# A mixture-of-experts block after a state-space layer: rows stored ready for the experts, and a start ordered around the first batch's norm

## The chip, the cores and the metric

The kernel runs on one core of a Trainium2 chip. A core has five engines with queues of their own: PE (matmuls), DVE (vector), ACT (scalar, with tables for functions), POOL (GpSimd) and SP (which only issues DMAs); PEld is PE's weight load. The metric is the device time of one execution in microseconds; less is better. A profile is one execution with its instructions recorded.

## The reference

All data are float32. x has 8 batches of 512 rows (tokens) with D = 256 features. A small matrix product of a condition `c` gives six vectors per batch: shift, scale and gate for each half of the layer.

```python
mod = (silu(c) @ wmod).reshape(8, 6, 1, 256)      # sa, ca, ga, sb, cb, gb
ga, gb: sign kept, magnitude at least 0.25
h = layernorm(x) * (1 + ca) + sa
# first half, a state-space layer with its own norm and residual
xn = layernorm(h) * gamma + beta
xp, z = split(xn @ W_in.T)                        # 512 + 512 features
xc = silu(causal_depthwise_conv(xp, 4 taps) + conv_b)
s_t = s_{t-1} @ A.T + xp_t @ Bm.T                 # 16 states, over the 512 rows
y = (xc + s @ Cm) * sigmoid(z)
x = x + ga * (h + y @ W_out.T)
# second half, eight experts, one for each token
h = layernorm(x) * (1 + cb) + sb
p = softmax(h @ wr + br); e = best expert; gate = p1 / (p1 + p2)
x = x + gb * gate * (gelu(h @ w1[e] + b1[e]) @ w2[e] + b2[e])
```

## The kernel before, in words

**Stages.** The first part goes over the eight batches. For each: `stage_norm` (both norms of x, then transposes to `xnT`, features on the partitions), `stage_base` (the residual `base` and the output weights `wb_` times the gate, both on POOL), `stage_conv` (the state scan by `pv`, `pd`, `v`, and the convolution: projections `px`, copies to `u`, three taps on DVE into `sv`), `stage_out` (projections for z, the states' part `pc`, then `po`: output projection and router logits together, giving the new x, `x1`), and `stage_place` (which expert, gate, and where among its expert's tokens each row goes: the row numbers are scattered to `ids_d` by indirect DMA). Ahead of the batches come general preparations: `states()` (powers of A and tables made of them, in many small matmuls and copies) and `vectors()` (the six vectors for all batches as rows, written to DRAM as `mod_d` and `modb_d`; by feature in `modT` through the tile `pf`; products of them with the router's weights). Batch 0's first three vectors are made apart, in `bc0`.

The second part goes over blocks of 256 rows of one expert (slots; some single ones of 128): weights `w1t`, `w2t`, biases `b1t`, `b2t`, the rows' numbers `ids`, and the rows `xg`, gathered from the DRAM table `xp_d` by indirect DMA. `features` makes the second norm's output `hg` on DVE and transposes it to `hT`; `layer1` gives `gl` by `ph` and Gelu; `layer2` gives `py`, then `ot` on DVE, which is scattered to the output. Four slots (`NEARLY`) are formed from the first six batches (`FEW`), and slot 0's rows and weights are fetched while the batches still run. The last three single slots run only if they are filled.

**A row of the table** holds 1028 numbers: the 256 of x1, the norm's 1/sigma and -mean/sigma, the gate, a zero (`OWN` = 260), then the batch's three vectors of the second half, which DMAs of 1.5 MB per batch copy from `modb_d` to every row, DRAM to DRAM.

**Order.** The kernel's text doesn't set the order of instructions. A class `Plan` records them, with estimated lengths, what each depends on, the buffers of its tiles and a due time (`nc.due`; `PERIOD` = 36 us a batch, `SLOT` = 14.5 us), passes due times back along dependencies, and then builds the queues in a loop that always takes the instruction that could start first, the earlier due one where two are equal:

```python
                    if best is None or (at, o["due"]) < best[:2]:
                        best = (at, o["due"], o)
```

What it takes is written out to the engines' queues in that order, and each queue runs strictly in order. `nc.wanting(done=...)` adds a dependency to the plan alone, `wanting([tile])` a buffer that must be free. There are two plans, one for each part. Line 154 is where a matmul that continues a group is recorded, line 159 any other instruction; so nearly all lines of the profile carry one of these two numbers, and tiles tell them apart.

**Other names.** `sv` (two buffers) holds the convolution and then y of a batch; `normed` is four ACT operations on [128, 256]; `stats` is bn_stats and bn_aggr on DVE, then `rs` by a power on POOL and `nm`; `late` (new) is a list of DMAs that the second part issues. The constant tables `sl_at`, `ex_at`, `seen` and `prio` are filled by one-element memsets on POOL.

Of the kernel before, what the change touches and what calls it, by code (L numbers as in the profile page):

```python
# [10 lines left out]
FP = mybir.dt.float32  # L11
# [10 lines left out]
OWN = 260  # L22
# [13 lines left out]
class Plan:  # L36
# [20 lines left out]
    def __init__(self, tc, last=None):  # L57

        self.tc, self.nc = tc, tc.nc
        self.free = {q: last.free[q] if last else 0.0 for q in self.REACH}  # L60
        self.ops, self.touched, self.tiles = [], {}, {}
        self.due, self.also, self.pairing = 0.0, ([], []), 0
        for name in self.QUEUES:
            setattr(self, name, self.Engine(self, name))
# [71 lines left out]
    def add(self, name, op, args, kw):  # L136
# [19 lines left out]
        else:  # L156
# [6 lines left out]
            self.ops.append(me)  # L163
        if op == "activation":
            me["table"] = {AF.Gelu: 1, AF.Silu: 2, AF.Tanh: 2}.get(args[2] if len(args) > 2 else None)
        if "dma" in op:
            me["size"] = 4
            for _, n in out.ap:
                me["size"] *= n
            me["indirect"] = "indirect" in op  # L170
# [20 lines left out]
    def order(self):  # L191
# [19 lines left out]
        order, table = [], 2  # L211
# [14 lines left out]
        while len(order) < len(ops):  # L226
            best = None
            for q, l in ready.items():
                for o in l:
# [6 lines left out]
                    if best is None or (at, o["due"]) < best[:2]:  # L236
                        best = (at, o["due"], o)
            assert best is not None, "no buffer for any instruction that could be next"
            at, _, o = best
            table = o.get("table") or table  # L240

# [6 lines left out]
            free[o["queue"]] = at + o["length"]  # L248
            end = at + o["length"]
# [40 lines left out]
def adaln_mamba_moe_kernel(  # L290
# [89 lines left out]
    for e in range(E):  # L380
        nc.gpsimd.memset(seen[0:1, e : e + 1], float(e * TOK))
# [4 lines left out]
    for i in range(NSLOT):  # L386
        single = i >= NPAIR
        m = i - NPAIR if single else i
        for q, v in enumerate((
            m, NPAIR + m // 2 if single else m, (m % 2) * P if single else 0,  # L390
            0 if single else NSING,
        )):
            nc.gpsimd.memset(sl_at[:, q, i : i + 1], float(v))

    ex_at = cpool.tile([1, 2, 2 * E], FP, name="ex_at")
    for e in range(2 * E):
        nc.gpsimd.memset(ex_at[:, 0, e : e + 1], float(e % E))
        nc.gpsimd.memset(ex_at[:, 1, e : e + 1], float((e % E) * TOK))
# [5 lines left out]
    ROW = OWN + 3 * D  # L404
    ids_d = dpool.tile([NIDS, 1], I32, name="ids_d")
    id_views = dram_disjoint_views(ids_d, NB)
    xp_d = dpool.tile([TOK + BLK, ROW], FP, name="xp_d")
# [6 lines left out]
    xg0 = epool.tile([P, JB, ROW], FP, name="xg0", tag="xg0")  # L414
    zero = xg0[:, 0, :]
# [15 lines left out]
    with tc.tile_pool(name="wa", bufs=1) as wa, tc.tile_pool(  # L431
# [3 lines left out]
    ) as a2, tc.tile_pool(  # L435
        name="rowp", bufs=2
# [27 lines left out]
        cmt = wa.tile([DS, DI], FP, name="cmt")  # L464
# [5 lines left out]
        for j in range(JB):  # L470
            nc.sync.dma_start(out=xp_d[TOK + j * P : TOK + (j + 1) * P, :], in_=zero)
# [41 lines left out]
        def vectors():  # L513

            for half, to in ((0, mod_d), (1, modb_d)):
                mod = wa.tile([B, 3, D], FP, name=f"mod{half}", tag="mod")
                three(mod, sT, half, B)
                nc.sync.dma_start(out=to, in_=mod.rearrange("b i d -> b (i d)"))


            pf = ps_o.tile([P, 6, B], FP, name="pf", tag="po")
            for m in range(6):
                w, at_m = (wmh[1], m) if m < 4 else (wmh[0], m)
                for k in range(KD):
                    nc.tensor.matmul(
                        pf[:, m], lhsT=w[:, k, at_m * P : (at_m + 1) * P],
                        rhs=sT[:, k, :], start=(k == 0), stop=(k == KD - 1),
                    )
            nc.vector.tensor_copy(modT[:, 0:2], pf[:, 0:2])
            nc.vector.tensor_scalar(modT[:, 2:4], pf[:, 2:4], 1.0, None, ALU.add)  # L530
            gT = modT[:, 4:6]
            nc.vector.tensor_copy(gT, pf[:, 4:6])
            mT = wa.tile([P, KD, B], FP, name="mT")
            nc.vector.scalar_tensor_tensor(mT, gT, -1.0, gT, ALU.mult, ALU.max)
            nc.vector.tensor_scalar(mT, mT, 0.25, None, ALU.max)
# [853 lines left out]
```

## Time and profile before

| | us |
|---|---|
| median of 3 runs | 591.7 (588.8 to 591.74) |
| the profiled execution | 587.33 |
| its span, first to last instruction | 585.2 |
| PE busy | 562.3 |
| DVE, ACT, POOL busy | 348.1, 211.0, 209.3 |
| first `po` of batch 0, of batch 7 (chain of waits) | 71.83, 305.51 |
| mean granted clock of PE | 0.987 |

In the page's rows of tenths each character is one of 40 equal slices of the span (14.6 us), 9 meaning 90% or more. In the windows view each engine has its busy microseconds and its count of instructions in brackets, then come the granted PE clock, the DMA share and GB/s. A timeline line has start, duration, engine, line, operation, tiles (out<-in), sizes and count, and in brackets the idle time before it and what ended it.

### The profile page before, as it was taken

Reading aid. Unit: us, or ns where it says so; the run is one execution under the profiler, and the core shown is the slowest. Engines: PE = TensorE matmul, PEld = TensorE weight load, DVE = VectorE, ACT = ScalarE, POOL = GpSimd, SP = SyncE. Lnnn points to the kernel's source line nnn. Section 1 sums busy time; section 2 is a strip of 40 time slices with the busy share of each in tenths; the row PEclk is TensorE's granted clock in tenths of the full one; section 3 lists DMA queues with packets and bytes.
Section 4 is the critical chain, followed back from the end, with each engine's and each line's share of the span. In section 5 each row is a group of like instructions: output and inputs, shape, how many; then the busy total and the mean of one; then the engine's idle time right before and its main releaser. Section 6 shows DMA issues by size and latency. Waiting matters only on the chain.

```text
span 585.2 us, 8673 instructions
## 1 busy us (share of the span) xinstructions
PE 562.3 (96%) x2882; PEld 428.0 (73%) x2882; DVE 348.1 (59%) x1087; ACT 211.0 (36%) x404; POOL 209.3 (36%) x330
## 2 busy tenths in 40 slices
PE   4999999999999999999999798999999999999996
PEld 2454766757576676757578687878988988988895
DVE  4879968798987968686595924163433433522312
ACT  2328454455363445252342021222422222332140
POOL 1423673635446372621333421342242222322112
PEclk9779999999999999999999999999999999999999
DMA  7348999420210101010553969997887787886000
GB/s 277 129 129 183 271 254 258 71 91 0 64 38 1 38 2 36 1 37 1 161 175 91 239 198 398 394 396 266 282 279 275 274 251 242 276 286 194 15 18 20
DMA packets 58703, 96.73 MB, mean 165 GB/s; under 512 B 9852, under 2 KB 41854, under 8 KB 58656
## 3 DMA queue, kind: packets, MB, share of 16 engines
q1 hardware_dynamic: 50720, 72.98, 41.4%
q0 software_dynamic: 7936, 23.17, 11.1%
q8 instruction: 24, 0.39, 0.3%
q14 instruction: 23, 0.19, 0.2%
HBM read 86.42 MB, written 22.81 MB: 187 GB/s over the span
## 4 chain that ended last, share of the span: by engine, by line
PE 73%; DMA 17%; DVE 3%; issue 3%; SPq 1%; POOL 1%; ACT 0%; POOLq 0%; ACTq 0%
PE py L154 10%; PE px L159 10%; PE po L154 9%; PE px L154 9%; DMA out<-ot,ids 8%; PE ph L159 6%; PE ph L154 6%; PE pc L154 3%; PE po L159 3%; PE pd L154 3%; DMA ids<-ids_d 3%; DMA ids_d<-tok,row 2%; DMA w1t<-in_w 2%; PE py L159 2%; DMA xg<-xp_d,ids 1%
## 5 line engine op out<-in xcount | busy, mean ns | idle before, releaser
L159 ACT ACTIVATE gl<-ph,b1t 128x256 f32<-128x256 f32 (+1 forms) x152 | 68.3, 452 | 179.5 <-PE ph L154 159.9
L154 PE MATMUL py<-w2t,gl 128*128 128x256 f32 x476 | 108.3, 379 | 0.0
L154 PEld LDWEIGHTS py<-w2t,gl 128*128 128x128 f32 x476 | 90.4, 190 | 12.3
L159 PE MATMUL ph<-hT,w1t 128*128 128x256 f32 (+1 forms) x304 | 84.1, 358 | 5.4 <-DMA w1t<-in_w 3.0
L154 PE MATMUL ph<-hT,w1t 128*128 128x256 f32 (+1 forms) x304 | 83.8, 357 | 0.0
L159 POOL DMA_INDIRECT out<-ot,ids x36 | 36.4, 1012 | 130.7 <-DVE ot L159 121.0
L159 DVE TENSOR_TENSOR ot<-py,b2t 128x256 f32<-128x256 f32 x34 | 14.4, 424 | 113.0 <-PE py L154 113.0
L159 DVE SCALAR_TENSOR_TENSOR sv<-u,pt,sv 128x512 f32<-128x512 f32 x96 | 71.9, 759 | 4.3 <-ACT sv L159 4.3
L159 POOL DMA_INDIRECT xg<-xp_d,ids x36 | 38.9, 1080 | 87.3 <-DMA ids<-ids_d 48.3
L159 PE MATMUL px<-xnT,wi 128*128 128x512 f32 x128 | 69.6, 625 | 0.0
L154 PE MATMUL px<-xnT,wi 128*128 128x512 f32 x128 | 66.2, 599 | 0.0
L159 PEld LDWEIGHTS ph<-hT,w1t 128*128 128x128 f32 x304 | 54.4, 190 | 12.2 <-issue 3.6
L154 PEld LDWEIGHTS ph<-hT,w1t 128*128 128x128 f32 x304 | 55.3, 190 | 6.2
L154 PEld LDWEIGHTS px<-xnT,wi 128*128 128x128 f32 x128 | 24.6, 192 | 31.2 <-issue 31.2
L159 POOL DMA_INDIRECT ids_d<-tok,row x32 | 34.5, 1077 | 24.2 <-DVE row L159 13.2
L159 ACT COPY u<-px 128x512 f32<-128x512 f32 x32 | 18.7, 585 | 67.0 <-PE px L154 66.4
L159 ACT ACTIVATE tz<-px 128x512 f32<-128x512 f32 x32 | 19.0, 595 | 51.1 <-PE px L154 50.3
L159 POOL TENSOR_TENSOR rs<-ve,nhalf 128x4 f32<-128x4 f32 x16 | 18.8, 1174 | 44.9 <-DVE ve L159 32.2
L159 PEld LDWEIGHTS px<-xnT,wi 128*128 128x128 f32 x128 | 21.3, 192 | 17.4 <-issue 16.5
L159 DVE COPY hT<-tp 128x512 f32<-128x512 f32 (+1 forms) x20 | 12.7, 634 | 35.4 <-PE tp L154 27.4
L159 DVE TENSOR_TENSOR xr<-po,h 128x256 f32<-128x256 f32 x32 | 13.5, 423 | 30.6 <-PE po L154 30.4
L159 DVE TENSOR_TENSOR hg<-hg,xg 128x256 f32<-128x256 f32 x72 | 29.3, 421 | 1.1
(347 smaller groups left out, 949.8 us busy)
## 6 DMA issues: line engine op xcount, KB each, us to landing
w1t<-in_w SPq DMA_DIRECT2D x19, 1024.0 KB
w2t<-in_w SPq DMA_DIRECT2D x19, 1024.0 KB
xp_d<-modb_d SPq DMA_DIRECT2D x8, 1536.0 KB
xp_d<-xr SPq DMA_DIRECT2D x8, 520.0 KB
xt<-in_x SPq DMA_DIRECT2D x8, 512.0 KB
bc<-mod_d SPq DMA_DIRECT2D x7, 384.0 KB
b2t<-in_b SPq DMA_DIRECT2D x19, 128.0 KB
w<-in_w SPq DMA_DIRECT2D x2, 1024.0 KB
```

Of the source, the lines that this page charges most:

```text
L154: me["calls"].append(lambda: getattr(getattr(self.nc, name), op)(*args, **kw))
L159: calls=[lambda: getattr(getattr(self.nc, name), op)(*args, **kw)],
```

## The change

- **What a row holds.** A row of `xp_d` becomes three times 256 numbers: x1, the second norm's finished output h2, and gg, which is gate times gb. They are made per batch in `stage_place`: h2 by four `normed` operations on ACT and two multiplications or additions of [128, 1024] on POOL, gg by four ACT operations; both lie in the batch's `sv`, which is now in a pool of its own (`yp`, two buffers). The three vectors come by one load `bb` per batch (one buffer). This work is due one `PERIOD` later than the rest of its batch. The last batch's h2 and gg are written by the second plan, behind slot 1's weights. The 1.5 MB copies of vectors go.
- **Experts.** `features` only transposes; `layer2` has two DVE operations on both tiles ahead of the matmuls and two per tile behind them, where there were three per tile. All four early slots are gathered in the first plan (there were two).
- **Start.** `stage_norm(0)` is recorded first, due at 20 us; `vectors()` is planned behind its `xnT`. `pf` is made by six transposes of `mod`'s rows, where there were 24 matmuls and seven DVE operations. Small copies in `states()` go from DVE to ACT.
- **Planner.** Up to 24 us (`hold`) an engine takes the earliest due of what could start within 0.3 us. Up to 100 us (`thick`) PE takes a dense instruction, if there is one within 0.3 us, when few columns were streamed in the last 3.4 us. Up to 20 us (`warm`) a PE that would wait gets filler matmuls of the identity, 256 columns each, into a tile that nobody reads.
- **Constants.** 116 one-element memsets become four iotas, some copies and some 15 memsets.

The diff, cut to its core:

```diff
@@ Plan.order
+                if could:
+                    mine = min(could)
+                    if mine[0] < self.hold:
+                        mine = min((c for c in could if c[0] < mine[0] + 0.3), key=lambda c: c[1:3])
+                    if q == "PE" and mine[0] < self.thick:
+                        t, l = mine[0], mine[3]["length"]
+                        lately = sum(
+                            d * max(0.0, b - max(a, t + l - 3.4)) / (b - a) for a, b, d in streamed[-40:]
+                        )
+                        if lately + mine[3]["dense"] < 1800:
+                            dense = [c for c in could if c[3]["dense"] > 900 * c[3]["length"] and c[0] < t + 0.3]
+                            mine = min(dense, key=lambda c: c[1:3]) if dense else mine
...
+            if self.warm and o["queue"] == "PE" and at < self.warm[0]:
+                slow = 2 if at < self.warm[1] else 1
+                n = int(0.8 * (at - free["PE"]) / (slow * self.warm[2]))
+                if n > 0:
+                    order.append(dict(i=-1, at=free["PE"], queue="PE", calls=[self.warm[3]] * n))
+                    streamed.append((free["PE"], at, 512 * n))
...
@@ vectors
+            pf = ps_o.tile([P, 6, B], FP, name="pf", tag="po")
             for half, to in ((0, mod_d), (1, modb_d)):
+                nc.due = (1 + 2 * half) * PERIOD
+                mod = rowp.tile([B, 3, D], FP, name=f"mod{half}", tag="bb", bufs=1)
                 three(mod, sT, half, B)
                 nc.sync.dma_start(out=to, in_=mod.rearrange("b i d -> b (i d)"))
+                for m, i in ((0, 1), (2, 0)) if half else ((4, 2),):
+                    for k in range(KD):
+                        nc.tensor.transpose(
+                            pf[:, m + k], mod[:, i, k * P : (k + 1) * P], ident[0:B, 0:B]
+                        )
+            nc.due = 3 * PERIOD
+            nc.vector.tensor_copy(modT, pf)
@@ states (and 13 more like it)
-                nc.vector.tensor_copy(at[:, j + 1], pa)
+                nc.scalar.copy(at[:, j + 1], pa)
@@ stage_place
+            own = xp_d[b * L : (b + 1) * L].rearrange("(n p) (i d) -> i p n d", p=P, i=3)
+            nc.sync.dma_start(out=own[0], in_=x1)
...
-            nc.sync.dma_start(
-                out=xp_d[b * L : (b + 1) * L, 0:OWN].rearrange("(n p) c -> p n c", p=P), in_=xr
-            )
-            for n in range(b + 1 if b else 0, min(b + 2, B)):
-                nc.sync.dma_start(
-                    out=xp_d[n * L : (n + 1) * L, OWN:ROW], in_=modb_d[n].partition_broadcast(L)
-                )
+            nc.sync.dma_start(
+                out=bb, in_=modb_d[b].rearrange("(i d) -> i d", d=D).partition_broadcast(P)
+            )
+            nc.due += PERIOD
+            normed(h2, x1, rs, nm)
+            nc.gpsimd.tensor_tensor(h2, h2, rows(bb[:, 0, :]), ALU.mult)
+            nc.gpsimd.tensor_tensor(h2, h2, rows(bb[:, 1, :]), ALU.add)
+            if b < B - 1:
+                nc.sync.dma_start(out=own[1], in_=h2)
+            for n in range(NT):
+                nc.scalar.activation(
+                    gg[:, n, :], bb[:, 2, :], AF.Identity, scale=gt[:, n, :]
+                )
+            if b < B - 1:
+                nc.sync.dma_start(out=own[2], in_=gg)
+            else:
+                late.extend(((own[1], h2), (own[2], gg)))
+            nc.due -= PERIOD
@@ features
-                nc.vector.tensor_scalar(
-                    hg[:, j, :], xg[:, j, 0:D], xg[:, j, D : D + 1], xg[:, j, D + 1 : D + 2],
-                    ALU.mult, ALU.add,
-                )
-                nc.vector.tensor_tensor(hg[:, j, :], hg[:, j, :], mg[:, j, 0:D], ALU.mult)
-                nc.vector.tensor_tensor(hg[:, j, :], hg[:, j, :], mg[:, j, D : 2 * D], ALU.add)
@@ the order of the start
+        plan.hold, plan.thick = 24.0, 100.0
+        plan.warm = (20.0, 7.8, 0.47, lambda: chip.tensor.matmul(
+            pwarm, lhsT=ident, rhs=twice, start=True, stop=True
+        ))
+        nc.due = 20.0
+        t = stage_norm(0)
+        nc.due = 1e6
         cs, wb, lm, bw = states()
-        rw, rsum, wr2 = vectors()
+        with nc.wanting(done=[t["xnT"]]):
+            rw, rsum, wr2 = vectors()
+            nc.due = 3 * PERIOD
+            stage_base(t)
@@ the early slots
+                for i in range(NEARLY):
+                    pre.append(rows_of(
+                        i, epool.tile([P, JB, 3, D], FP, name=f"xg_{i}", tag=f"xg{i}"), (b + 1) * L
+                    ))
@@ the second plan
+        for to, v in late:
+            with nc.wanting(done=[got[1][4]]):
+                nc.sync.dma_start(out=to, in_=v)
@@ layer2
+            nc.vector.tensor_tensor(
+                ot[:, 0:jb], gg, b2t.unsqueeze(1).to_broadcast([P, jb, D]), ALU.mult
+            )
+            nc.vector.tensor_tensor(x1, x1, ot[:, 0:jb], ALU.add)
...
-                nc.vector.tensor_tensor(ot[:, j, :], py, b2t, ALU.add)
-                nc.vector.tensor_tensor(ot[:, j, :], ot[:, j, :], mg[:, j, 2 * D : 3 * D], ALU.mult)
-                nc.vector.scalar_tensor_tensor(
-                    ot[:, j, :], ot[:, j, :], xg[:, j, D + 2 : D + 3], xg[:, j, 0:D],
-                    ALU.mult, ALU.add,
-                )
+                nc.vector.tensor_tensor(ot[:, j, :], py, gg[:, j, :], ALU.mult)
+                nc.vector.tensor_tensor(ot[:, j, :], ot[:, j, :], x1[:, j, :], ALU.add)
```

## The prediction

> **What bounds the kernel now.** I read the page first: which engine is full, and in which slices.
>
> ```profile
> span 585.2 us, 8673 instructions
> PE 562.3 (96%) x2882; PEld 428.0 (73%) x2882; DVE 348.1 (59%) x1087; ACT 211.0 (36%) x404; POOL 209.3 (36%) x330
> ...
> PE   4999999999999999999999798999999999999996
> ...
> PEclk9779999999999999999999999999999999999999
> DMA  7348999420210101010553969997887787886000
> ```
>
> PE is full almost everywhere, so only three things can pay: PE work removed, PE time at a low granted clock, and the few slices below 9 (the first, the 23rd and 24th, the last). The PEclk row has two sevens right at the start. Next the windows view, cut by stage, to see what those places are worth.
>
> ```profile
> core 0: us, PE busy (x) PEld busy (x) DVE busy (x) ACT busy (x) POOL busy (x), PEclk, DMA share, GB/s
> 0.00:10.00 10.00, 2.60 (x17) 0.93 (x17) 5.45 (x34) 1.50 (x2) 2.73 (x24) 1.00 0.74 262
> 10.00:20.00 10.00, 10.00 (x57) 6.32 (x56) 6.19 (x23) 3.15 (x6) 0.10 (x1) 1.00 0.88 330
> 20.00:30.00 10.00, 10.00 (x42) 3.05 (x42) 7.79 (x27) 4.51 (x8) 7.05 (x7) 0.66 0.01 2
> 30.00:40.00 10.00, 9.11 (x33) 5.82 (x32) 8.65 (x34) 1.95 (x3) 3.09 (x9) 0.70 0.53 141
> 40.00:50.00 10.00, 10.00 (x58) 4.95 (x56) 6.84 (x17) 6.26 (x10) 3.93 (x3) 0.95 0.61 146
> ...
> 80.00:313.00 233.00, 231.47 (x1220) 156.77 (x1213) 184.54 (x593) 103.78 (x182) 101.35 (x192) 1.00 0.26 70
> 313.00:345.00 32.00, 28.81 (x142) 24.71 (x141) 21.19 (x102) 7.36 (x17) 13.01 (x13) 1.00 0.74 183
> 345.00:388.00 43.00, 39.75 (x187) 33.77 (x186) 15.72 (x37) 11.38 (x24) 13.73 (x14) 1.00 1.05 383
> 388.00:550.00 162.00, 162.00 (x818) 143.99 (x817) 60.10 (x148) 45.81 (x102) 44.60 (x42) 1.00 0.76 256
> ```
>
> From 80 to 313 us (the batches) PE idles 1.5 us in 233; from 388 to 550 (the experts) not at all. DVE is at 79% in the batches and 37% in the experts, so DVE work taken from the experts' stage buys nothing there. What is left is the start (0 to 80) and the hand-over between the stages (313 to 388), where PE idles 6.4 us and DMA stands at 0.74 and 1.05. Last, the timeline of the start: when do inputs land, and when does batch 0 reach its projections?
>
> ```profile
> 5.64 1.41 DVE L159 BATCH_NORM_STATS2 st<-xt 128x6 f32<-128x256 f32 x4 [1.21 <-DMA xt<-in_x]
> 9.98 2.08 PE L159 MATMUL pm<-wm,s 128*128 128x512 f32 x2
> 10.20 0.14 DVE L159 SCALAR_TENSOR_TENSOR nm<-mv,rs 128x4 f32<-128x4 f32 x1
> 24.24 2.07 ACT L159 ACTIVATE xn<-h,nm,rs 128x256 f32<-128x256 f32 x4 [1.63 <-DVE nm L159]
> 37.48 2.05 PE L159 MATMUL px<-xnT,wi 128*128 128x512 f32 x2
> ```
>
> x of batch 0 is there at 5.6 us, its second norm ends at 26.3, yet the first projection starts at 37.5: PE spends the time between on general preparations. And two 128x512 matmuls take 2.05 to 2.08 us here; their median in the tile's own rows is 592 ns each, overlapping. They run at half rate.
>
> **The change part by part.**
>
> *Start, clock.* PEclk of 0.66, 0.70 and 0.95 in the three windows from 20 to 50 us is 0.34+0.30+0.05 of 10 us: 6.9 us of PE lost. The record says 1.00 before 20, but pm at 9.98 runs at half speed too; dense work began at 7.97 and pg of 15.09 us is fast again, so another 2 to 3 us. The change puts filler matmuls on the waiting PE from about 2 us (ident is ready at 1.7), and up to 100 us of the plan prefers dense PE work when the last 3.4 us were thin. The Trainium skill (TensorE: Matmul & The Clock Gate, Part 1) says that the ramp penalty is under 1% of a typical span and should not be fitted: by the rule under 5.9 us, paid once. The trace shows the clock falling back twice more, 6.9 plus about 2.5 us, 1.6% of the span. I go by the trace: 9.4 us to be had. Fillers run only where the planner expects an idle PE; a misjudged input costs one batch of fillers, 1 to 2 us.
>
> *Start, PE work.* pf loses 24 matmuls (2.6 us, of 16.05 to 18.80) for six small transposes; the start-to-start of tp transposes is 0.11 us, so 0.7: 1.9 us gained. Together 11.3 us of PE time.
>
> *Start, order.* Batch 0's norm is due first. By the rows above: stats to 7.6, rs on POOL 1.04, nm at 8.9 (no longer behind a copy of `at`: it went at 10.20 because that copy waited for PE), xn 2.1, two h operations 2.4, stats and rs 3.8, xn 2.1, transposes and xnT 2: projections from about 22 us instead of 37.5. That alone is worth nothing, since PE was busy; it lets dense work fill the stretch in which it was thin. All of `vectors()` now waits for xnT in the plan: mod_d, written at 33.3, may come later by some us, and batch 1's bc with it; batch 1's projections are not needed until 80, so this is covered by 40 us.
>
> *Start, other engines.* 35 copies of 16x16 to 128x128 size go from DVE to ACT: 35 x 0.155 = 5.4 us off DVE, and about 35 x 0.2 (the row of gt, 128x4, 0.20 us) = 7 us onto ACT. DVE was at 10.00 and 9.61 of 10 from 50 to 70 us, behind the sv taps, and a start that is 11 us shorter gives it less time: 53 us of DVE work from 10 to 80 become about 47 in 58. It fits, but not without bubbles. 116 one-element memsets of POOL at 0.09 us (10 us) go; nobody waited for them: nothing. I take 8 of the 11.3 us, bounds 2 and 13.
>
> *Batches.* Per batch, normed(h2) adds four ACT operations (2.07 us by the row of xn) and gg four more (2.1): ACT from 103.8/233 = 45% to 57%. POOL gets two multiplications of 128x1024, 2.35 us each by the rows of h: 43% to 58%. Nobody on PE waits for h2 or gg of the same batch. What is queued behind them: on POOL the ids_d scatters and the next base, on ACT u and sv copies, each late by one operation at most, 0.5 us (ACT) or 2.35 (POOL). But DVE and POOL share a port. The row is
>
> ```profile
> 28.83 2.41 POOL L159 TENSOR_TENSOR h<-h,xt 128x1024 f32<-128x1024 f32 x1
> ...
> 28.95 2.31 DVE L159 COPY lx<-more 16x16 f32<-16x16 f32 x1
> ```
>
> a 16x16 copy that takes 0.155 elsewhere and here lasts as long as the POOL operation. The skill (SBUF — State Buffer, Who interferes with whom) says the loser blocks fully until the other ends: by the rule 16 x 2.35 = 37.6 us of DVE could go, 4.7 per batch. Over the 24 such POOL operations of this trace I add up the excess of each overlapped DVE operation over its usual length: 15.8 us, 0.66 each. I take 16 x 0.66 = 10.6 us on DVE, 1.3 a batch: 79% becomes 84%, still below PE. To PE passes what falls into the scan (v, pd, v), where PE waits for DVE: I take +1 us, bounds 0 and +10.6.
>
> SP: per batch the 1536 KB DRAM broadcasts and the 520 KB rows become three writes of 512 KB and a 384 KB load. The broadcasts held SP's queue for 30 us from 42.7 and DMA at 1.02 from 60 to 80, but nothing on PE waited: nothing. sv is now held until h2 and gg are written (see rivals).
>
> *Hand-over.* PE's idle stretches here, by the timeline: 0.99 (w1t of slot 1), 2.21 (ACT waiting for b1t), 2.04 (w1t of the third weights, 12.4 us under way at DMA 1.05) and 1.1 in bits at 383 to 387 (rows of slot 4). Rows of slots 2 and 3 (four gathers of 526 KB, 2.1 MB) move ahead of 313, into a stage with DMA at 0.26; each later gather is a quarter smaller; against it, 1 MB of h2 and gg of the last batch comes in after slot 1's weights instead of a 520 KB write. Net over 1.5 MB less at 383 GB/s: 4 us of transfer. But h2 of the last batch needs ACT 2.1 and POOL 4.7 behind the four scatters that end at 327.6: about 333; SP stands in order before it, while slot 4's ids load waits for ids_d until 340.4 anyway, 7 us of cover. I take -2 us, bounds -5 and +4.
>
> *Experts and tail.* Of DVE six operations of a two-tile slot leave features and two leave layer2, and two that span both tiles come: covered by PE at 162 of 162, nothing; with the cover gone it would be 2 to 3 us a slot. Only behind the last py does one stand free: three operations (0.42+0.42+0.48) become two, -0.5.
>
> Sum: -8 +1 -2 -0.5 = -9.5, from the profiled execution's 587.33 (span 585.2): 577.8. The median shown, 591.7, is 4.4 above that execution; from it the same gain gives 582.2.
>
> **The rivals.**
>
> *A: PE keeps the whole start.* Only the clock and pf count, nothing is lost to DVE, the hand-over closes: -11.3 -5 -0.5 = -17, about 575. For it: 9.4 us are recorded. Against it: DVE at 10 of 10 from 50 to 70.
>
> *B: the start is given back in the batches.* If the port's price goes through to PE (+10.6) and the start brings 8, the sum is -8+10.6-2-0.5 = 0: 591.8, no change. For it: 14 DVE operations were caught in this trace, one tap for 2.78 us. Against it: those cost PE 1.5 us in 233.
>
> *C, slower: sv is held too long.* Two buffers; conv of batch b+2 needs the one of b, 33.4 us after the last po of b (first po at 71.83 for batch 0 and 305.51 for batch 7 in the chain of waits: 233.7/7). h2 and gg are due one PERIOD (36) later than the rest of their batch, so they run last. Ready when nothing stands ahead: x1 and rs 4 us, normed 2.1, POOL 4.7, write and landing 4: 15 us. It decides from 33 us on: then PE waits, and with 36 us it is 3 us for six batches, +18, and the whole +8.5: 600. For it: POOL at 58% with in-order queues. Against it: engines take what is ready, and 18 us of slack.
>
> *D: the fillers and the dense rule do nothing* (the gate falls anyway): then -1.9 and the order, about -3 with the hand-over: 589.
>
> **How the numbers follow.** The sum 0.50, A 0.15, B with D 0.15, C and its like 0.20. A measurement here tells about 0.5% (3 us) from no change. Faster: the sum, A and a third of B/D: 0.70. Same: 0.09. Slower: C and B's upper bound, 0.21. The range: 573 (A) up to 597, within C, leaves out about 2 in 10. The likeliest case alone is 577 to 588.
>
> **What would show it.** PEclk at 0.95 or above in all windows from 10 to 50 us; the first px near 22; last po of batch 0 (now 77.9) near 70, and later ones still 33 to 34 us apart; DVE at 82 to 86% in the batches; idle PE of 313 to 388 near 4 us; the last slot shorter by 0.5. It is wrong if po of batch 0 is not earlier than 75, if px waits for sv's write, or if the batches are over 34.5 us apart.

## The result, and the profile after

The changed kernel takes 627.0 us (623.53 to 628.53, four runs); in the same comparison the kernel before took 590.25 (585.69 to 591.74). The ratio is 1.0628, 95% interval 1.055 to 1.0706. The forecast said 582.2 and at most 597: it was wrong in sign and in size. The page of the kernel after, the rows that answer to those shown of before:

```profile
span 625.5 us, 8602 instructions
...
PE 577.2 (92%) x2876; PEld 438.5 (70%) x2876; DVE 354.0 (57%) x938; ACT 243.9 (39%) x503; POOL 252.4 (40%) x246
...
PE   7799998878989889799799898799999999999996
...
PEclk9787998998999979899999999999999999999999
DMA  8231124933122257201335989999787678686000
```

The kernel before had nines in PE's row from slice 2 to 22; now there are sevens and eights among them, and the clock falls again and again. From slice 27 to 39 there are nines again, as before. (Lines 153 and 158 are here what 154 and 159 are in the kernel before; other runs have a neighbouring pair.) The windows view, cut at the first `po` of batch 0 and of batch 7, puts numbers to it. Before, then after:

```profile
70.20:304.80 234.60, 233.03 (x1230) 157.94 (x1231) 183.34 (x596) 106.80 (x190) 108.04 (x198) 1.00 0.30 79
304.80:585.20 280.40, 268.36 (x1338) 235.74 (x1338) 110.04 (x318) 73.76 (x163) 76.24 (x73) 1.00 0.69 229
```

```profile
0.00:74.10 74.10, 66.44 (x328) 37.19 (x329) 58.61 (x153) 39.13 (x96) 31.94 (x60) 0.86 0.36 121
74.10:345.10 271.00, 243.96 (x1216) 165.64 (x1215) 209.91 (x567) 127.72 (x237) 140.73 (x114) 0.95 0.37 70
345.10:625.50 280.40, 266.83 (x1336) 235.71 (x1334) 85.53 (x220) 77.04 (x170) 79.69 (x73) 1.00 0.71 223
```

The part behind the batches takes 280.40 us in both. The seven batch periods between took 234.6 and now take 271.0: +36.4. The columns account for it. PE idles 271.00 - 243.96 = 27.0 us where it idled 1.6: +25.4. And PE is busy 243.96 us where it was 233.03, with 14 matmuls fewer: +10.9. The two are the whole 36.4. A mean clock of 0.95 over 271 us, where it was 1.00, is up to 13.6 us of PE's work, and so covers the second part. Two thirds of the loss are waits of PE, one third is a lower clock. DVE's busy time rose by 26.6 us with fewer instructions. Who makes PE wait is in its waits (us in total, times, longest):

```profile
PE pk L153 <- DVE sx L158: 10.8, 5, 4.0
PE pd L158 <- DVE v L158: 6.7, 6, 3.0
PE px L153 <- issue: 3.2, 1, 3.2
```

The third belongs to a standstill of several engines in the second period, which the last section shows. Why DVE is late in the others is in the timeline around the longest one:

```profile
215.75 5.36 POOL L158 TENSOR_TENSOR sv<-sv,bb 128x1024 f32<-128x1024 f32 x2 [5.37 <-ACT sv L158]
...
215.84 2.31 DVE L158 TENSOR_SCALAR gt<-gt 128x4 f32<-128x4 f32 x1
...
217.61 0.30 PE L158 MATMUL pk<-oh,lower 128*128 128x32 f32 x2
218.07 0.15 DVE L158 TENSOR_TENSOR sx<-sx,oh 128x8 f32<-128x8 f32 x1
...
218.81 2.31 DVE L158 TENSOR_TENSOR sx<-sx,oh 128x8 f32<-128x8 f32 x1
...
221.91 0.64 PE L153 MATMUL pk<-sx,ones 128*128 128x32 f32 x2 [4.00 <-DVE sx L158]
```

The multiplication and the addition that make h2 run on POOL from 215.75 to 221.11. Under each of them one tiny DVE operation lasts 2.31 us. The second one is a sum that places rows; its twin at 218.07 takes 0.15 us, while this one ends at 221.12, together with POOL's. PE's second `pk` waits for that sum, and what comes next on PE's queue waits in order behind `pk`.

### The profile page after: what moved, and what is told of

Its sections match the earlier page's. It is cut to its first block, busy times and chain, and to the rows that moved or that the text cites. A ratio compares the mean times of both kernels' runs of the same rounds, so it can differ in the third digit from the quotient of the medians.

```text
span 625.5 us, 8602 instructions
## 1 busy us (share of the span) xinstructions
PE 577.2 (92%) x2876; PEld 438.5 (70%) x2876; DVE 354.0 (57%) x938; ACT 243.9 (39%) x503; POOL 252.4 (40%) x246
## 4 chain that ended last, share of the span: by engine, by line
PE 49%; DVE 25%; DMA 15%; issue 4%; POOL 3%; SPq 2%; another core or an unknown queue 2%; ACT 1%; POOLq 0%; DVEq 0%
PE py L153 12%; DVE sv L158 8%; DMA out<-ot,ids 7%; PE ph L158 6%; PE ph L153 6%; PE po L153 5%; DVE h L158 4%; PE px L158 4%; PE px L153 3%; DVE sx L158 3%; PE pc L153 3%; DMA w<-in_w 3%; DMA w1t<-in_w 2%; DVE st L158 2%
## 5 line engine op out<-in xcount | busy, mean ns | idle before, releaser
L158 DVE TENSOR_TENSOR ot<-py,xg 128x256 f32<-128x256 f32 x36 | 15.3, 424 | 126.2 <-PE py L153 124.9
L158 DVE SCALAR_TENSOR_TENSOR sv<-u,pt,sv 128x512 f32<-128x512 f32 x96 | 75.1, 791 | 4.8 <-ACT sv L158 4.1
L158 PE MATMUL px<-xnT,wi 128*128 128x512 f32 x128 | 74.9, 669 | 0.3 <-DVE sv L158 0.3
L153 PE MATMUL px<-xnT,wi 128*128 128x512 f32 x128 | 70.8, 637 | 3.2 <-issue 3.2
L158 POOL DMA_INDIRECT xg<-xp_d,ids x36 | 41.3, 1146 | 66.6 <-DMA ids<-ids_d 22.0
L158 PEld LDWEIGHTS ph<-hT,w1t 128*128 128x128 f32 x304 | 54.8, 190 | 11.9 <-issue 6.1
L158 POOL TENSOR_TENSOR sv<-sv,bb 128x1024 f32<-128x1024 f32 x16 | 41.1, 2572 | 36.8 <-ACT sv L158 29.7
L153 PEld LDWEIGHTS px<-xnT,wi 128*128 128x128 f32 x128 | 26.3, 206 | 37.6 <-issue 37.5
L158 POOL TENSOR_TENSOR rs<-ve,nhalf 128x4 f32<-128x4 f32 x24 | 29.9, 1246 | 39.4 <-DVE ve L158 34.8
L158 DVE COPY hT<-tp 128x512 f32<-128x512 f32 (+1 forms) x20 | 12.7, 634 | 40.9 <-PE tp L153 36.1
L158 PEld LDWEIGHTS px<-xnT,wi 128*128 128x128 f32 x128 | 21.9, 199 | 16.5 <-issue 14.3
L158 DVE TENSOR_TENSOR x<-po,h 128x256 f32<-128x256 f32 x32 | 13.5, 423 | 34.0 <-PE po L153 25.6
L158 DVE TENSOR_TENSOR sv<-sv,pc 128x512 f32<-128x512 f32 x32 | 21.4, 682 | 19.7 <-PE pc L153 16.9
```

Source lines behind the costliest of these rows:

```text
L153: me["calls"].append(lambda: getattr(getattr(self.nc, name), op)(*args, **kw))
L158: calls=[lambda: getattr(getattr(self.nc, name), op)(*args, **kw)],
```

## The experiments

They answer four questions. A ratio is to the kernel before, timed beside it on the same chip (medians from 585.41 to 588.32). "The batches" are the time from the first `po` of batch 0 to that of batch 7.

### Which part of the change costs?

**The start alone**: the kernel before with the planner's rules, fillers, batch 0's norm first, the vectors behind it, copies on ACT, constants by iota; rows and experts as before.

> The kernel before with the start part alone: the planner's hold, thick and fillers, batch 0's norm first, vectors from transposed rows, small copies on ACT, iotas; rows, gathers and experts as before. Theory 1 (the loss lies in the batches, by what is added to them per batch; the start gives nothing, since first po of batch 0 came at 74.1 against 70.2 while 3.5 us more of batch 1's projections stood before it): 585 to 593 us, within 1% of before, po to po 32 to 35 us. Theory 2 (the start's order and the planner's rules cost the batches their time): 605 us or more, periods of 36 us and above.

614.54 us, ratio 1.0483 (1.0434 to 1.0532): neither theory, for the time is that of the second, but the periods are not. One hole makes the loss. From `po` to `po`, the second period is 61.4 us long, the others 30 to 35. In its timeline:

```profile
155.57 0.43 DVE L160 BATCH_NORM_STATS2 st<-xt 128x6 f32<-128x256 f32 x1 [25.37 <-DMA xt<-in_x]
156.64 0.80 PE L160 MATMUL pc<-v,cs 128*128 128x128 f32 x2 [23.71 <-DVE sv L160]
```

DVE's queue stands at the statistics of an x that is not there, and everything behind them stands too. SP's lines say why x is late:

```profile
73.11 0.30 SPq L160 DMA_DIRECT2D modb_d<-mod  x1
74.75 28.00 SPq L160 DMA_DIRECT2D xp_d<-modb_d  x7
102.79 22.23 SPq L160 DMA_DIRECT2D bc<-mod_d  x1
```

The second half of the vectors was written at 36.4 us before and at 73.1 here, so the DRAM copies of 1.5 MB per batch run beside the loads of the batches. The complete change has no such copies, so this hole is not its own.

**The rows alone**: the changed kernel without the start part (three tiles share buffers for room).

> The change without its start part: rows of x1, h2 and gg, early gathers, the new layer2; the order of the start, the planner's rule and the constants as before (two tables and the vectors' rows share buffers as in the changed kernel, for space). Theory 1 (the added work per batch costs it all): 618 to 630 us, periods of 36 to 40 us. Theory 2 (the start's rules cost it): under 600 us.

635.74 us, ratio 1.0808 (1.0749 to 1.0868); all periods are 36 to 45 us. The rows carry the loss; beside 627.0 the start takes 9 us off it, as far as a run with shared buffers can tell.

**h2 on DVE.**

```diff
-            nc.gpsimd.tensor_tensor(h2, h2, rows(bb[:, 0, :]), ALU.mult)
-            nc.gpsimd.tensor_tensor(h2, h2, rows(bb[:, 1, :]), ALU.add)
+            nc.vector.tensor_tensor(h2, h2, rows(bb[:, 0, :]), ALU.mult)
+            nc.vector.tensor_tensor(h2, h2, rows(bb[:, 1, :]), ALU.add)
```

> The changed kernel with h2's multiplication and addition on DVE where they were on POOL: two DVE operations of 1.2 us a batch more, 16 POOL operations of 2.57 us fewer. Theory P (the POOL operations hold the port that DVE needs: 13 DVE operations caught, 27.7 us in excess, one of them twice a batch the sx that PE waits for): DVE's excess falls from 45 to about 17 us, PE's waits for sx go, 598 to 610 us. Theory J (DMA packets of several us while row numbers are scattered and h2 and gg are written, during which every engine stands): under 6 us faster than the changed kernel, 620 us or more.

599.95 us (597.29 to 605.47), ratio 1.0244 (1.0169 to 1.0319). Of the 37 us lost, 23 (by the ratios) to 27 (by the medians) came back by moving sixteen operations to the fuller engine. The group of lines and the window of this kernel:

```profile
L158 DVE TENSOR_TENSOR sv<-sv,bb 128x1024 f32<-128x1024 f32 x16 | 19.4, 1215 | 0.0
```

```profile
73.80:318.20 244.40, 236.42 (x1216) 159.87 (x1215) 199.31 (x582) 125.85 (x238) 110.99 (x101) 0.97 0.46 86
```

DVE takes 19.4 us of new work and its busy sum still falls, from 209.91 to 199.31. PE's idle time falls from 27.0 to 8.0 us. Not all of this need be caught operations: 12.7 of the 26.6 us by which the batches get shorter lie in the second period (47.5 us in the changed kernel, 34.8 here), and the standstill in it is gone too.

**Other writes.** h2 and gg not written; instead x1 three times, early.

> The changed kernel with the writes of h2 and gg (all batches but the last) replaced by two writes of x1 of the same size, issued together with x1's own as soon as x1 is there, 15 to 20 us ahead of the scatters of row numbers; h2 and gg are still made, but rows of the table hold x1 in their place, so the router's and experts' inputs differ only in values. Theory J: no packets over 2 us in the batches, no common stand of the engines (118 to 126 us), period 2 down from 47.5 to 36: 605 to 615 us. Theory P: stands go only in part, sx still waits; 618 us or more.

623.32 us, ratio 1.0613 (1.0547 to 1.0678): 4 us by the medians, 1 by the ratios, within the noise. That is what the moment of the writes, and holding `sv` for them, is worth. What the writes cost as such is not shown, since as many bytes are written here.

### What does h2 on POOL cost with?

**Quarters**: each of the two operations as four of 128x256.

```diff
+            for n in range(NT):
+                nc.gpsimd.tensor_tensor(h2[:, n, :], h2[:, n, :], bb[:, 0, :], ALU.mult)
+                nc.gpsimd.tensor_tensor(h2[:, n, :], h2[:, n, :], bb[:, 1, :], ALU.add)
```

> The changed kernel, with each of h2's two POOL operations of 128x1024 cut into four of 128x256, order and amount of work as near as can be. Theory P1 (a POOL operation of two inputs shuts DVE out for as long as it lasts, so a caught DVE operation pays its rest): a catch now costs at most about 0.65 us instead of 2.5, but there are four times as many operations to be caught by; the DVE excess falls from 45 us to about 35 and the longest single waits of PE on sx and v from 4.0 to about 2, so 612 to 620 us. Theory P2 (what costs is the sum of POOL's time with the port, in whatever pieces): no change, 625 to 629. Theory Q (POOL's queue: what stands behind h2 there is late): no change either, or slower by the overhead of more instructions, 627 to 635.

618.04 us, ratio 1.055 (1.0472 to 1.0629), as P1 said. The waits of its PE between 70 and 345 us:

```profile
PE pd L158 <- DVE v L158: 7.6, 9, 3.9
PE pk L153 <- DVE sx L158: 6.8, 5, 1.9
```

POOL is busier than in the changed kernel (159.90 against 140.73 us in the batches, more instructions), yet PE idles 17.5 us there instead of 27.0. It is the length of the single operation that DVE pays, not POOL's sum. The sign of it is the waits at `pk` (10.8 us, the longest 4.0, are now 6.8, the longest 1.9), not the time: 5.0 of the 6.1 us by which the batches get shorter lie in the second period, whose standstill is missing here too.

**Two POOL operations in the kernel before**, everything else unchanged:

```diff
+            nc.due += PERIOD
+            k0, k1 = sv[:, 0:KD, :], sv[:, KD : 2 * KD, :]
+            nc.gpsimd.tensor_tensor(k0, k0, k1, ALU.mult)
+            nc.gpsimd.tensor_tensor(k0, k0, k1, ALU.add)
+            nc.due -= PERIOD
```

> The kernel before, with two more POOL operations of 128x1024 per batch, on its own sv once y has been used, due one PERIOD later like h2's (their result isn't read by anything; nothing else is changed: no new DMA, no new ACT work). Theory P (h2 on POOL costs through the port): the batches become 3 us longer each, 608 to 618 us. Rival C' (most of the loss comes from the writes and loads of rows, ACT's eight more operations and sv held until its rows have landed): under 4 us, 588 to 594.

631.24 us, ratio 1.0752 (1.069 to 1.0814). The batches:

```profile
72.50:334.80 262.30, 244.97 (x1230) 162.52 (x1231) 212.32 (x597) 106.01 (x190) 142.42 (x174) 0.95 0.24 68
```

262.3 us against 234.6: +27.7, about what moving h2 off POOL gave back, with no new row, write or ACT operation. There is no standstill in this run, and each of the seven periods is longer, by 1.3 to 5.1 us. DVE's busy time rises by 29.0 us with one instruction more; under the two operations twelve DVE operations in the batches last 19.6 us longer than usual. No engine waits for `sv` from POOL there. (The other 19 us lie behind the batches: SP issues three loads of `ids` only at 396.55 us, behind the weights of slots, and PE waits 12.5 us for the rows.) Its timeline shows how the queue passes a catch on to PE:

```profile
241.14 3.49 DVE L159 SCALAR_TENSOR_TENSOR sv<-u,pt,sv 128x512 f32<-128x512 f32 x2
241.74 2.35 POOL L159 TENSOR_TENSOR sv<-sv 128x1024 f32<-128x1024 f32 x1
244.04 2.79 POOL L159 TENSOR_TENSOR wb__683<-wo,bc 128x1024 f32<-128x1024 f32 x1
244.55 2.30 DVE L159 SCALAR_TENSOR_TENSOR xr<-mv,xr 128x4 f32<-128x4 f32 x1
...
247.81 0.27 DVE L159 TENSOR_TENSOR v<-v,pd 32x127 f32<-32x127 f32 x1
...
248.13 0.60 PE L159 MATMUL pd<-v,lm 32*32 32x120 f32 x2 [4.43 <-DVE v L159]
```

Neither caught operation is one that PE waits for. But `v` stands behind both on DVE's queue, and PE waits for `v`.

**POOL busy without reading**: four memsets in the place of those two operations.

```diff
-            nc.gpsimd.tensor_tensor(k0, k0, k1, ALU.mult)
-            nc.gpsimd.tensor_tensor(k0, k0, k1, ALU.add)
+            for _ in range(4):
+                nc.gpsimd.memset(k0, 0.0)
```

> The kernel before with four POOL memsets of 128x1024 per batch on its own sv, after y has been used, where the earlier run had two operations of two inputs; nothing reads them. Theory port (two-input POOL operations shut DVE out; a memset reads nothing and does not): DVE's excess in the batches stays near 8 us, the periods stay at 33 to 35 us, 587 to 592 in all. Theory queue (POOL being busy for 4 to 5 us more per batch delays rs, the scatters and base): as with the two operations, 610 to 630.

619.81 us, ratio 1.0605 (1.0552 to 1.0658), which taken alone would speak for the queue. The profile speaks against it. The group and the batches:

```profile
L159 POOL MEMSET sv<- 128x1024 f32 x32 | 30.6, 956 | 9.8 <-PE po L154 9.8
```

```profile
69.90:307.80 237.90, 234.02 (x1231) 158.17 (x1232) 191.53 (x597) 107.09 (x190) 130.03 (x170) 1.00 0.28 77
```

30.6 us of POOL work, against 39.6 with the two operations, and the batches are 3.3 us longer instead of 27.7; no DVE operation is caught under a memset. Nearly the whole loss, 27.2 us of the span, lies behind the batches, at the same place as in the run above: three `ids` loads behind weights, a wait of 13.4 us, and a lower clock. What puts those loads so late in both runs is not shown; POOL's longer queue may. In the batches, then, POOL's time is not what costs, but POOL's reading of two inputs while DVE works. A POOL operation with one input was not tried.

**h2 on POOL, due at once.**

```diff
-            nc.due += PERIOD
...
-            nc.due -= PERIOD
```

> The changed kernel, h2 still on POOL, but h2 and gg due with their batch and not one PERIOD later. Theory P (a POOL operation costs what the DVE work under it delays; with the delay they lie beside the next scan and the placing chain sx, which PE's queue waits for): at once they lie beside the router's small operations of the same batch, which are on the same chain; the catches move but do not go, 615 to 635 us. Rival (it is the due time that was wrong): under 605.

632.38 us, ratio 1.0768 (1.0706 to 1.0831): the catches move (waits for `v` 13.8 us, longest 7.3; for `sx` 6.2), they do not go.

### How does a wait of 1.3 us cost 3 us?

In the run with quarters PE waits 1.29, 1.28 and 1.29 us at `pk` from 175.25, 212.56 and 249.94 us, and the trace has the clock at half for 3.4 us from 178.4, 216.0 and 253.5: each of these waits is followed, some 3 us after it began, by a loss of another 1.7 us. Not every wait is: in the changed kernel one of 1.79 us at `pk`, up to 299.22, is followed by no half clock. The test fills the waits:

```diff
+            pk_ = ps_t.tile([P, NT * E + 2 * P], FP, name="pk", tag="tp")
+            for _ in range(5):
+                nc.tensor.matmul(pk_[:, NT * E :], lhsT=ident, rhs=twice, start=True, stop=True)
```

> The changed kernel with h2 in quarters (618.0), and five filler matmuls of 256 columns per batch in PE's queue ahead of pk, where PE waits 1.1 to 1.9 us for sx in seven batches and the clock is halved for 3.4 us some 3 us later. Theory K (a thin stretch of PE, wait and small matmuls, is what lowers the clock): half clock in the batches falls from 34 us to under 18, the waits at pk go, and the time is 608 to 613. Rival (the clock falls for another reason, or the fillers cost what they save): half clock as before, 617 to 625.

617.83 us, ratio 1.0537 (1.0487 to 1.0587).

```profile
72.40:341.50 269.10, 253.53 (x1303) 173.65 (x1302) 207.86 (x576) 130.65 (x243) 160.94 (x157) 0.97 0.28 78
```

Half clock in the batches falls from 34 to 13.6 us, and the three falls above are gone, so a thin PE around the wait is what lowered the clock there. The time does not fall: the batches are 4 us longer. PE waits nowhere at `pk` now, but idles 15.6 us in all where it idled 17.5 (8.9 at `pd`, and 4.7 at `pc` for `row`, which is new), and the fillers' own time comes on top. The cause is shown; it is no cure.

### Where did the start's 8 us go, and is there a better version?

**The start alone, modb_d early**, so that the copies stand where they stood:

```diff
-                nc.due = (1 + 2 * half) * PERIOD
+                nc.due = PERIOD
```

> The kernel before with the start part alone, as in the run of the start before, but the second half of the vectors is due as early as the first, so that modb_d is written near 40 us and the broadcasts of vectors to rows stand where the kernel before has them. Theory S (the start is worth what I forecast, -8, and the 23.7 us hole was the price of the late broadcasts): 580 to 584. Theory N (the start gains nothing, since the clock still falls and PE waits elsewhere): 587 to 592.

589.33 us, ratio 1.0046 (1.0026 to 1.0065). The hole is gone, and with it the whole loss, but nothing is gained. The first `po` of batch 0 comes 2.5 us earlier (67.7), that of batch 1 0.4 us earlier (104.5 against 104.9). Two runs take the start further apart, without the fillers and without the rules on order:

> The start alone (with modb_d early), without the filler matmuls. Theory F (the fillers hold the clock up early and what falls later falls for other reasons): PEclk falls once more before 20 us and the run is 2 to 4 us slower than with fillers, 591 to 594. Theory G (the fillers buy nothing: the gate falls at 17 us anyway, and PE has its small preparations to do in either case): equal to the run with fillers within 1.5 us, 588 to 590.

> The start alone (with modb_d early) with fillers, but without the two rules that reorder what an engine takes next (earliest due within 0.3 us up to 24 us, dense PE work up to 100 us). If the rules do what the forecast supposed: more half clock before 80 us and 590 to 593. If they only move work from batch 1 into the start and leave batch 1 thinner (first period 36.8 us in the run with them): first po of batch 0 later, the first period shorter, and 586 to 589 in all.

592.13 us (1.0042 to 1.0116 around 1.0079) and 593.0 us (1.006 to 1.0169 around 1.0114). By the ratios the fillers are worth 2 us and the rules 4; the intervals of all three runs overlap, so neither is sure. Up to the first `po` the clock still costs 5.1 us with both, 6.8 without fillers and 10.2 without the rules; in the kernel before it was 6.8.

**The cheaper work alone** (copies on ACT, six transposes for `pf`), **the planner's part alone**, and **the fillers alone**, each on the kernel before:

> The kernel before with the start's cheaper work alone: small copies of states() on ACT and pf by six transposes instead of 24 matmuls and seven DVE operations. No new order, fillers or rules, no change to constants. My forecast's own term for this work was -1.9 on PE and 5.4 us less on DVE: 583 to 586. If the start is bound by the order of what arrives and PE has other work anyway: 587 to 590.

> The kernel before with the planner's part of the start alone: fillers to 20 us, earliest due within 0.3 us up to 24 us, dense PE work up to 100 us; work, order of the text and rows as before. If the clock can be held by filling and choosing (the 6.8 us lost to it in the start of the kernel before): half clock before 80 us falls from 13.6 us to under 7, and 580 to 584. If PE's work in the start is thin whatever is chosen: half clock as before, 585 to 590.

> The kernel before with the filler matmuls alone. They can only fill PE's waits of the first 8 us (2.6, 1.5 and 3.4 us). If that holds the clock up beyond 20 us: 583 to 585. If not: 585 to 588, and the first half clock merely comes at another time.

624.79 us (ratio 1.0683), 615.81 (1.0486), 611.67 (1.0452): all far from every expectation, and all by the hole of the first experiment. With the fillers alone:

```profile
65.83 0.29 SPq L160 DMA_DIRECT2D modb_d<-mod  x1
```

```profile
132.35 0.43 DVE L160 BATCH_NORM_STATS2 st<-xt 128x6 f32<-128x256 f32 x1 [19.85 <-DMA xt<-in_x]
```

In these runs modb_d is written at 67.3, 62.3 and 65.8 us, and PE has one gap of 15.2, 18.7 and 15.5 us at 114 to 142 us. None of them has a due time for the vectors, so any shift in the plan lets them slip. They therefore give no answer on the start's terms, but for one: with the fillers alone the first `po` comes at 65.0 us, 5.2 us earlier than before. How much of that is the fillers' and how much the vectors that moved behind it is not shown; fillers with modb_d held early, on the kernel before, were not tried.

**Three attempts at the rest of the loss with h2 on DVE.** That run had two long periods, the fourth of 37.4 us and the seventh of 40.9. In the fourth, ACT waits for the write of the rows that still holds `sv` (rival C's mechanism); in the seventh the power for `rs` stands behind gathers on POOL:

```profile
190.38 0.78 ACT L158 ACTIVATE sv<-px,pt 128x512 f32<-128x512 f32 x1 [4.43 <-DMA xp_d<-sv]
191.21 1.13 PE L158 MATMUL px<-xnT,wi 128*128 128x512 f32 x2 [2.45 <-ACT sv L158]
...
294.07 1.07 POOL L158 DMA_INDIRECT xg<-xp_d,ids  x1 [18.36 <-DMA ids<-ids_d]
295.44 1.00 POOL L158 DMA_INDIRECT xg<-xp_d,ids  x1 [0.31 <-issue]
296.48 1.05 POOL L158 TENSOR_TENSOR rs<-ve,nhalf 128x4 f32<-128x4 f32 x1
```

First both cures together (rows due at once, two early gathers); then the vectors early with neither; then the gathers alone:

```diff
-                for i in range(NEARLY):
+                for i in range(2):
                     pre.append(rows_of(
```

> The changed kernel with h2's two operations on DVE, h2 and gg due with their batch instead of one PERIOD later, and only two of the four early slots gathered in the first plan, as before. Theory C (in the run with h2 on DVE alone, what was left of the loss came from sv's rows landing late, period 4, and from the gathers of slots 2 and 3 standing ahead of rs on POOL, period 7): both holes go, 586 to 591 us. Rival (the rows simply add DVE and ACT work of 3 to 4 us a batch that a nearly full DVE passes on): 597 to 603.

> The changed kernel with h2 on DVE, and both halves of the vectors due at one PERIOD. If the start loses its gain to the late second half of the vectors, the first po of batch 0 comes at 68 to 70 us instead of 73.8 and the whole is 594 to 597; if the vectors do not matter here (no broadcasts are left to collide), 598 to 602.

> The changed kernel with h2 on DVE, due one PERIOD later as in the change, but only two of the four early slots gathered in the first plan. If the seventh period of 40.9 us came from the gathers that wait on POOL ahead of rs: that period is 33 to 34 us, first po of batch 7 at 311 instead of 318, and the hand-over gives back 2 to 4 us: 593 to 597. If something else made it: 598 to 602.

602.2 us (ratio 1.0262), 607.25 (1.0344) and 594.15 (1.0151, interval 1.0109 to 1.0193). Rows due at once cut PE's wait behind `sv` to 1.4 us, but gave others (`pc` for `v`, 5.0 us in four): that theory fell. Early vectors brought the first `po` to 67.0 us, and then a second period of 43.0. Only the gathers alone helped, though the seventh period fell to 37.0 us and not to 33 or 34:

```profile
74.80:312.80 238.00, 230.96 (x1216) 157.37 (x1215) 199.11 (x582) 126.08 (x238) 106.82 (x97) 1.00 0.44 82
```

238.0 us of batches, PE idle 7.0, no lost clock. It is the best form of the whole change, and still 1.5% slower than the kernel before. No version run here beats the kernel before.

## Why the prediction was wrong, point by point

- **Batches, +1 with bounds 0 to +10.6: measured +36.4.** This is the step that failed, in two terms. *The price of a catch.* I took 0.66 us for each new POOL operation, the mean over the 24 of the trace before, and set aside the rule of the Trainium skill (SBUF — State Buffer, Who interferes with whom: the loser blocks fully), which gave an estimate of 37.6 us. In the trace after, the sixteen h2 operations caught thirteen DVE operations for 27.7 us, 2.1 each. The mean was the wrong row: between 70 and 345 us the eighteen POOL operations of that kind had caught only eight DVE operations, while h2, due one period later, meets the placing sums `sx`, eight of its thirteen catches. The rule was much nearer: it gave a third more than was measured. *What passes to PE.* I took a tenth of DVE's delay. PE's and DVE's queues are in order, so what stands behind `pk` and `pd` waits too: PE idles 25.4 us more, 17.5 us of it at these two, and the lower clock adds 10.9. "84% is still below PE" argued from an average and overlooked both. How much of the 36.4 the standstill of the second period makes is open; the run with two POOL operations has none and loses 27.7.
- **Rival B** had the right mechanism and a third of the size. **Rival C** did not decide in the changed kernel; no engine waits for the rows' write there. It appears when h2 is on DVE: ACT then waits 10.5 us for it in five waits, the longest 4.43.
- **Start, -8: measured about zero.** The order came as forecast: first `px` at 24.0 us, forecast near 22. But PEclk from 10 to 50 us is 0.77, 0.84, 0.70 and 1.00, not 0.95 and above, and once the projections are early PE waits elsewhere:

```profile
29.38 0.27 PE L158 MATMUL pf<-ident,mod 8*128 8x8 f32 x1 [3.22 <-DVE mod L158]
```

  I took the clock's 9.4 us for a thing that fillers remove. They fill waits of the first 8 us; of the falls, that at 15.4 us comes with PE busy on small matmuls, and that at 29.1 at the end of the wait of 3.2 us above. The Trainium skill's "under 1%" (TensorE: Matmul & The Clock Gate, Part 1), which I set aside, does not describe this kernel either: 0.14 of 74.1 us and 0.05 of 271 are 24 us, 4% of the span. But setting it aside gave me a loss to win back, not a way to do so. The first `po` of batch 0 came at 74.1 instead of 70.2 us. With h2 off POOL that of batch 1 stands at 105.5 against 104.9: the start neither gains nor loses. Only beside the rows did it show 9 us, against a run that had to share buffers.
- **The vectors "covered by 40 us"** holds in the changed kernel. In the kernel before, with its copies, the same slip costs 15 to 24 us (four runs): I had called those copies "nothing" since nobody on PE waited for them where they stood.
- **Hand-over, -2: nothing.** Behind the first `po` of batch 7 PE idles 13.6 us in 280.40, before 12.0 in as many; the waits are now for `w1t`, 5.5 us in two.
- **Experts, 0: right.** DVE has 24.5 us less to do behind the batches, and the time is the same. **Tail, -0.5:** one operation fewer behind the last matmul, and 0.2 us less from there to the end.
- **DVE 82 to 86% in the batches:** 209.91 of 271 is 77%, because the stretch itself grew; the sum was the sign to watch, and it rose by 26.6 where I had 10.6.

## What to carry to other kernels

Before work goes to an idle POOL, look at what DVE does at that moment: a two-input POOL operation of 2.4 us makes one short DVE operation under it last as long, and an in-order PE that waits on that DVE's queue pays it too, and here once more in clock. Cost such a move by the operation's length times the catches on a chain that PE waits for, not by a mean over the trace. And a transfer that nobody waits for is free only where it stands: what happens if it slips by a period belongs in the sum.

## What the hardware showed that I had not expected

- A POOL memset of 128x1024 takes 0.96 us and caught no DVE operation in 32 cases; a two-input operation of that size takes 2.34 us or more, and h2's sixteen caught thirteen.
- Waits of PE of 1.3 us, among small matmuls, can be enough for half clock: 3.4 us of it some 3 us later in three cases, none after a wait of 1.79 us.
- In the changed kernel a 512 KB write and a 384 KB load issued at 106.31 and 106.76 us, just behind the 4-byte scatters, have packets of 1024 bytes that take up to 14.09 us. Then DVE, ACT and POOL stand, and PE for 3.21 us up to 126.22:

```profile
126.33 2.35 POOL L158 TENSOR_TENSOR wb__444<-wo,bc 128x1024 f32<-128x1024 f32 x1 [7.75 <-remote]
126.34 0.42 DVE L158 TENSOR_TENSOR x<-po,h 128x256 f32<-128x256 f32 x1 [8.24 <-remote]
126.56 0.58 ACT L158 COPY u<-px 128x512 f32<-128x512 f32 x1 [11.87 <-remote]
```

What they wait for the profile does not name. Such a standstill, at the same place and 3.7 to 11.9 us for the engine that stands longest, is in each of the four runs that write rows and make h2 in whole operations on POOL, and in none of the six with h2 on DVE or in quarters. Long packets alone do not make it: with the rows due at once engines stand up to 10.4 us and no packet takes over 5.7; with quarters one takes 10.8 us and nothing stands. Writing the rows earlier shortens it to 3.7 us. The second period is 47.5 us with it, and 40.6 in the run with two POOL operations and no rows; by that estimate it costs about 7 us. Its cause stays open.
